# Transposing the convolved tiles of a state-space layer on VectorE and through memory instead of on TensorE

## The chip, the core and the metric

The kernel runs on one core of a Trainium2 chip. A core has TensorE (matrix products, with a queue for loading weights, PEld), VectorE (DVE), ScalarE (ACT), GpSimd (POOL) and SyncE (SP), which here issues nearly all DMA transfers from one queue; transfers are moved by 16 DMA engines. Matrix products are accumulated in PSUM, which has eight banks of 128 x 512 floats; everything else lies in SBUF. Each engine works through its own list of instructions in order, and waits at an instruction until what it needs is there. The metric is the time of one execution on the device in microseconds; lower is better. The text gives the median of several executions.

## What is computed

Two layers on `x` of shape (2, 512, 512): each adds `s * silu(f)` to `x`, where `s` is an attention-like part and `f` a feed-forward part. The change lies in the attention-like part of the second layer, a Mamba-2 block with 128 heads of 64 channels in 8 groups, state size 128 and chunks of 128 time steps:

```python
hBC = silu(causal_conv(hBC, conv_w, conv_b))         # 4 taps along time
hid, B, C = split(hBC)                               # hid: 128 heads x 64
hid_dt = hid * dt[..., None]
A_cs = cumsum(A * dt)                                # within a chunk
L = exp(segsum(A * dt))
M = einsum('cihn,cjhn->cijh', C, B) * L
Y_diag = einsum('cijh,cjhp->cihp', M, hid_dt)
states = einsum('clhn,hcl,clhp->chpn', B, exp(A_cs[-1] - A_cs), hid_dt)
prev_states = ...                                    # states carried from chunk to chunk
Y_off = einsum('clhn,chpn,hcl->clhp', C, prev_states, exp(A_cs))
y = (Y_diag + Y_off + Dp * hid) * silu(gate)
y = y * rsqrt(mean over the group of y*y + eps) * gnorm_w
out = x + y @ out_proj.T
```

The projections and the convolution are made with channels on the partitions and time along the row, since the taps run along time. The products with `M` and the sums for the states run over time, so they want `hid * dt` with time on the partitions. Between the two each 128 x 512 tile must be transposed, in four blocks of 128 x 128. That transpose is what is changed.

## The kernel before

The first 530 us make the first layer, the feed-forward parts, and the tables that the block needs. The rest (L1048 to L1985) is one loop over 64 steps, written out by hand in order: the program is recorded in the order of the Python calls, so the place of a call fixes the place of its instructions in each engine's list.

The work is cut into 16 units (group g, batch b; `u = 2g + b`) of 8 tiles each; a tile is 128 channels (two heads) by 512 time steps. A step handles two tiles, so a unit has four steps, called t = 0, 2, 4, 6 by the first tile's place in its unit. In step d four pairs of tiles are at work:

- `a` (tiles 2d, 2d+1): `products` (L1171), the two big sums with `M` and with the states; then `finish_y` (L1199) on VectorE (L1205, L1206).
- `n` (tiles 2d+2, 2d+3): the transposes on TensorE (`transposed`, L1226), the scaling by dt and by the decay (`values`, L1233: `hc` for the products, `hcd` for the states), the exponentials (`clamp` and `decays`, L1249 to L1269), the moments with B (`begun`, L1271, tile `pn`), the states of the four chunks (`states`, L1281: one copy on ScalarE, then four small VectorE instructions), and C times the decay on GpSimd (`starts`, L1299, tile `eb`).
- `h` (tiles 2d+4, 2d+5): projected on TensorE by a seven-product scheme (class `Values`), convolved on ScalarE and VectorE (`first_tap`, `taps`), then a silu on ScalarE (`silu`, L1589) at the end of the step, because silus and exponentials need a table load on ScalarE between them.
- `p` (tiles 2d-2, 2d-1): multiplied by the gate's silu on GpSimd (L1688) and squared (`square`, L1210: ScalarE squares, GpSimd adds).

At t = 0 the next unit's B and C are projected and convolved (`inner`); at t = 4 B is transposed on TensorE and multiplied with C (`inner_products`). In a unit's steps t = 2, 4, 6 the output product of the unit before is made on TensorE (class `Output`; VectorE adds each piece to `acc`, L1553, and the next piece goes into the same bank). For it GpSimd makes four sums of y (L1498) at t = 2 ahead of `starts`, and four at t = 4 behind them. The weights of the output are loaded once in a group (`load_out`, 2 MB, at t = 0 of a b = 1 unit), and four long sums of them are made on GpSimd (`sum_out`, L1093 to L1098): two at t = 0 and two at t = 2 of the b = 1 unit. At the end of a step GpSimd makes eight sums of the weights of the next step's projections (L581).

Loads for a step are issued on SP at its start, in this order: `load_sums` for two tiles (`cs`, which waits until the products have released a buffer), `load_starts` (`eb`), `load_gate` (`wg`), `load_hid` (`wh`), then `load_rest` (`el`).

The eight PSUM banks are: `pj` three (projections and gates), `tr` one (transposes, moments, B's transposes), `de` one (the exponentials), `of` one and `yy` two (output, products and others). The transposed tile is read by `values` right out of PSUM; the scale factors lie in SBUF.

## Time and profile before

Three runs took 2213.21, 2215.6 and 2215.95 us; the median is 2215.6 us. The profiled execution has a span of 2213.2 us, and its time is the same to the digit given, 2213.2. The granted TensorE clock is 1.000 throughout.

| engine | busy us | share of the span | instructions |
|---|---|---|---|
| TensorE | 2191.3 | 99% | 12460 |
| VectorE | 1513.8 | 68% | 2985 |
| ScalarE | 1299.4 | 59% | 2864 |
| GpSimd | 1321.7 | 60% | 1234 |

From 530 us on, in the loop, TensorE is busy 1675.2 of 1683 us, VectorE 1229.6, ScalarE 1151.2, GpSimd 1132.3, and the DMA engines 49%.

How to read it: in a line of a timeline stand the start in us, the time in us, the engine, the source line, the operation, the tile written and the tiles read, the shape, and how many instructions are merged; in square brackets the idle time before it and who ended it. Names are without their buffer numbers: `px` is a transposed tile in PSUM, `pjh` a projection of a tile, `gt` and `gty` of a gate, `of` and `ofy` an output product, `py` the products, `cs` the sums that become exponentials, `de` their bank, `s` and `wt` the sums for the output. A recorded time includes the end of the pipeline, so that the next instruction of an engine can start a little before the one ahead ends; start to start is what an instruction holds its engine.

### The profile page before, as it was taken

The numbers are of one execution on the slowest core, as the hardware profiler recorded it, in microseconds if no ns is written. First come the engines' busy times: TensorE is split into PE (matmuls) and PEld (weight loads), VectorE is DVE, ScalarE is ACT, GpSimd is POOL, SyncE is SP. The second block draws the span as 40 slices with busy tenths as digits, with TensorE's granted clock in tenths as the row PEclk, the third lists the DMA queues.
The fourth block names the chain that finished last, engine by engine and source line by source line (L and its number), as shares of the span: only waits on it lengthen the run. The fifth ranks groups of instructions, "written<-read, shape, count | busy, mean of one in ns | idle before, by whom it ended". The sixth has DMA issues, their size and how long they took to land.

```text
span 2213.2 us, 35453 instructions
## 1 busy us (share of the span) xinstructions
PE 2191.3 (99%) x12460; PEld 1712.6 (77%) x12460; DVE 1513.8 (68%) x2985; ACT 1299.4 (59%) x2864; POOL 1321.7 (60%) x1234
## 2 busy tenths in 40 slices
PE   8999999999999999999999999999999999999999
PEld 4545567765568888888888888888888888888877
DVE  5263577545777777777777677777777677777763
ACT  4131323214777667676767676767767676767671
POOL 4151523323457567776766686759576866766577
PEclk9999999999999999999999999999999999999999
DMA  4012266755544446444545454454446444544452
GB/s 174 1 58 75 80 226 221 255 195 195 176 143 129 148 140 190 133 135 124 167 133 148 152 175 128 134 162 129 134 141 187 138 145 124 167 124 133 141 187 97
DMA packets 195953, 323.51 MB, mean 146 GB/s; under 512 B 17728, under 2 KB 129984, under 8 KB 193344
## 3 DMA queue, kind: packets, MB, share of 16 engines
q1 hardware_dynamic: 189376, 300.28, 44.5%
q0 software_dynamic: 6400, 20.98, 2.5%
q8 instruction: 99, 1.62, 0.3%
q14 instruction: 78, 0.64, 0.1%
HBM read 294.45 MB, written 26.74 MB: 145 GB/s over the span
## 4 chain that ended last, share of the span: by engine, by line
PE 95%; DVE 2%; ACT 1%; DMA 1%; POOL 0%; issue 0%; SPq 0%; ACTq 0%; DVEq 0%
PE pjh L607 15%; PE of L1530 15%; PE gt L607 13%; PE py L1177 5%; PE pjbc L1139 5%; PE pf L1018 4%; PE pn L1276 4%; PE py L1186 4%; PE px L1230 3%; PE ofy L1530 2%; PE hu L361 2%; PE sh L522 2%; PE pg L607 2%; PE pu L607 2%; PE gty L607 2%; PE gt L1139 2%
## 5 line engine op out<-in xcount | busy, mean ns | idle before, releaser
L1301 POOL TENSOR_TENSOR eb<-CT,eb 128x768 f32<-128x768 f32 x128 | 230.0, 1818 | 342.9 <-DMA eb<-ea_d 287.1
L1254 ACT ACTIVATE cs<-cs,sl 128x128 f32<-128x128 f32 x1024 | 325.0, 390 | 0.6 <-DMA cs<-cs_d 0.6
L1158 DVE SCALAR_TENSOR_TENSOR hid<-pjh,cw,hid 128x511 f32<-128x511 f32 (+2 forms) x384 | 286.5, 746 | 43.1 <-ACT hid L1149 35.6
L1269 DVE TENSOR_TENSOR cs<-de,CB 128x512 f32<-128x512 f32 x256 | 175.4, 685 | 80.0 <-ACT de L1268 79.0
L1688 POOL TENSOR_TENSOR y<-y,sgt 128x512 f32<-128x512 f32 x124 | 176.1, 1440 | 11.6 <-ACT sgt L1410 9.7
L1177 PE MATMUL py<-cs,hc 128*64 128x128 f32 x2048 | 180.3, 276 | 0.0
L1222 POOL TENSOR_TENSOR sums<-sums,sq 128x512 f32<-128x512 f32 x110 | 140.1, 1273 | 61.3 <-ACT sq L1218 57.6
L1268 ACT ACTIVATE de<-cs 128x512 f32<-128x512 f32 x256 | 154.0, 602 | 28.9 <-DVE cs L1269 22.6
L1186 PE MATMUL py<-eb,st 128*64 128x128 f32 x1536 | 149.1, 273 | 0.0
L1289 DVE SCALAR_TENSOR_TENSOR st<-st,sl,pn 128x64 f32<-128x64 f32 x512 | 108.4, 275 | 59.4 <-ACT st L1285 59.4
L1553 DVE SCALAR_TENSOR_TENSOR acc<-of,rg,acc 128x256 f32<-128x256 f32 x188 | 90.2, 480 | 74.7 <-PE of L1530 74.4
L1354 ACT COPY hid<-pjh 128x256 f32<-128x256 f32 x171 | 63.6, 372 | 129.5 <-PE pjh L607 127.7
L1206 DVE SCALAR_TENSOR_TENSOR y<-hid,Dcol,y 128x512 f32<-128x512 f32 x128 | 133.8, 1045 | 4.5
L1177 PEld LDWEIGHTS py<-cs,hc 128*64 128x64 f32 x2048 | 121.5, 137 | 19.9 <-issue 18.1
L1205 DVE TENSOR_TENSOR y<-py,el 128x512 f32<-128x512 f32 x128 | 87.7, 685 | 57.1 <-PE py L1186 56.3
L1285 ACT COPY st<-pn 128x128 f32<-128x128 f32 x128 | 33.1, 264 | 153.3 <-PE pn L1276 153.3
L1530 PE MATMUL of<-wt,y 128*128 128x256 f32 x512 | 121.8, 381 | 0.0
L1139 PE MATMUL pjbc<-hT,wbc 128*128 128x512 f32 x256 | 117.4, 593 | 2.1 <-DVE BT L1158 1.3
L1530 PE MATMUL of<-wo,s 128*128 128x256 f32 x496 | 118.8, 382 | 0.0
L1276 PEld LDWEIGHTS pn<-hcd,Bs 128*128 128x128 f32 x768 | 104.7, 191 | 16.5 <-issue 11.3
L607 PE MATMUL pjh<-th,sh 128*128 128x256 f32 x456 | 117.3, 380 | 0.2 <-POOL sh L581 0.2
L607 PE MATMUL pjh<-hT,wh 128*128 128x256 f32 x456 | 117.2, 379 | 0.0
(356 smaller groups left out, 5518.7 us busy)
## 6 DMA issues: line engine op xcount, KB each, us to landing
cs<-cs_d SPq DMA_DIRECT2D x128, 512.0 KB, 4.3
eb<-ea_d SPq DMA_DIRECT2D x256, 192.0 KB, 6.0
wh<-in_in_wT SPq DMA_DIRECT2D x64, 512.0 KB, 9.2
wg<-in_in_wT SPq DMA_DIRECT2D x64, 512.0 KB, 7.4
el<-ea_d SPq DMA_DIRECT2D x256, 128.0 KB, 7.5
wo<-wo_d SPq DMA_DIRECT2D x16, 1024.0 KB, 8.4
wop<-in_out_wT SPq DMA_DIRECT2D x39, 256.0 KB, 2.8
wo_d<-wop POOLq DMA_DIRECT2D x39, 256.0 KB, 2.8
```

The costliest lines, as they stand in the source:

```text
L607: nc.tensor.matmul(ps, x[:, k, :], y[:, k, :], start=(first and k == 0), stop=(k == 1), skip_group_check=True,)
L1139: nc.tensor.matmul(ps, w_of(k), hT[:, k, bass.ts(b, S)], start=(k == 0), stop=(k == KD - 1))
L1158: nc.vector.scalar_tensor_tensor(dst[:, j:], ps[:, : S - j], cw[:, ct, KCONV - 1 - j : KCONV - j], dst[:, j:], ALU.mult, ALU.add,)
L1177: nc.tensor.matmul(py[bass.ts(hh, HP), bass.ts(c, P)], hc[:, c, bass.ts(hh, HP)], M[:, hh, bass.ts(c, P)], start=True, stop=(c == 0),)
L1186: nc.tensor.matmul(py[bass.ts(hh, HP), bass.ts(c, P)], st[:, c - 1, bass.ts(hh, HP)], cte[:, hh, bass.ts(c - 1, P)], start=False, stop=True,)
L1254: nc.scalar.activation(m[:, bass.ts(c, P)], m[:, bass.ts(c, P)], AF.Relu, bias=sls[g][:, 3, b * NCH + c, h0 + hh : h0 + hh + 1], scale=-1.0,)
L1268: nc.scalar.activation(pe, m, AF.Exp, scale=-1.0)
L1269: nc.vector.tensor_tensor(m, pe, CBs[s // GT].rearrange("p c i -> p (c i)"), ALU.mult)
L1276: nc.tensor.matmul(pn[:, c, :], Bss[s // GT][:, c, :], hcd[:, c, :], start=True, stop=True)
L1301: nc.gpsimd.tensor_tensor(eb_t[s], CTs[s // GT][:, P:].unsqueeze(1).to_broadcast([P, 2, S - P]), eb_t[s], ALU.mult,)
L1530: nc.tensor.matmul(ps, x[:, k, :], y[:, k, :], start=(first and k == 0), stop=(k == 3), skip_group_check=True,)
L1688: nc.gpsimd.tensor_tensor(y_of(s), y_of(s), sgs.pop(s), ALU.mult)
```

## The change

For all tiles but the first two, the transposes on TensorE are taken away. `turn` stands in their place, behind the silus of the step before: VectorE transposes the tile in blocks of 32 x 32 (one instruction for a tile of 128 x 512), which leaves each block in its band of 32 partitions; four DMA stores per pair, one for each band, write the blocks to their places in a scratch tensor in memory (pieces of 512 bytes), and in the next step `fetch` loads the pair back (pieces of 2 KB) into the tile it came from. The pair shares one SBUF tile with the squares (`sq`), which were two tiles before. `values` reads the tile from SBUF now, and because of the layout it takes four instructions instead of two. It stands later in VectorE's list, behind two exponentials' multiplies. The four VectorE instructions of the second tile's states move behind the transposes. B's transposes stay on TensorE. The bank `tr` is gone and `de` has two banks, which the exponentials, the moments, B's transposes and the mean of squares take in turn; two exponentials of a tile are issued one after the other on ScalarE, and their multiplies apart from them. On SP, `fetch` stands behind the `cs` loads, and `load_starts` and `load_out` move behind `fetch`, `load_gate` and `load_hid`.

```diff
+        def two_tiles(name):
+            return wk.tile([P, 2, S], F32, tag="sq", name=name, bufs=1)
+
+        def turn(ss, between=None):
+            if ss:
+                to = two_tiles(f"tn{ss[0]}")
+                for j, s in enumerate(ss):
+                    nc.vector.transpose(
+                        to[:, j, :].rearrange("p (q c e) -> p q c e", q=4, c=NCH),
+                        hid[s].rearrange("p (c q e) -> p q c e", c=NCH, q=4),
+                    )
+                    raw[s] = to[:, j, :]
+                    if between and j == 0:
+                        between()
+                dst = dram.tile([2, P, 4, P], F32, tag="tn_d", name=f"tn_d{ss[0]}", bufs=3)
+                for a in range(4):
+                    nc.sync.dma_start(
+                        dst[:, :, a, :].rearrange("j (q r) e -> r j q e", q=4),
+                        to[32 * a : 32 * a + 32].rearrange("r j (q e) -> r j q e", q=4),
+                    )
+                sent[ss[0]] = to, dst
+
+        def fetch(ss):
+            if ss:
+                to, src = sent.pop(ss[0])
+                nc.sync.dma_start(to, src.rearrange("j p a e -> p j (a e)"))
...
-                q = wk.tile([P, S], F32, tag="sq", name=f"sq{s}", bufs=2)
+                q = pairs[0][:, t % 2, :]
...
-            for dst, j, n in ((hc, 0, NCH), (hcd, 1, NCH - 1)):
-                nc.vector.tensor_tensor(
-                    dst.rearrange("p c (h d) -> p c h d", h=2),
-                    pxh[:, 0:n],
-                    pair(sls[g][:, j, b * NCH : b * NCH + n, h0 : h0 + 2]),
-                    ALU.mult,
-                )
+            for dst, j, n in (
+                (hc.rearrange("p c (a e) -> p a c e", a=4), 0, NCH),
+                (hcd.rearrange("p c (a e) -> p a c e", a=4), 1, NCH - 1),
+            ):
+                for h in range(2):
+                    two = slice(2 * h, 2 * h + 2)
+                    f = sls[g][:, j, b * NCH : b * NCH + n, h0 + h]
+                    f = f.unsqueeze(1).unsqueeze(3).to_broadcast([P, 2, n, 32])
+                    nc.vector.tensor_tensor(dst[:, two], src[:, two, 0:n], f, ALU.mult)
...
-            pe = psum.tile([P, S], F32, tag="de", name=f"de{s}_{hh}", bufs=1)
+            pe = psum.tile([P, S], F32, tag="de", name=f"de{s}_{hh}", bufs=2)
             nc.scalar.activation(pe, m, AF.Exp, scale=-1.0)
-            nc.vector.tensor_tensor(m, pe, CBs[s // GT].rearrange("p c i -> p (c i)"), ALU.mult)
+
+            def multiplied():
+                CB = CBs[s // GT].rearrange("p c i -> p (c i)")
+                nc.vector.tensor_tensor(m, pe, CB, ALU.mult)
+
+            return multiplied
...
-            tag, bufs = ("pj", 3) if spare else ("tr", 1)
+            tag, bufs = ("pj", 3) if spare else ("de", 2)
             pn = psum.tile([P, NCH - 1, P], F32, tag=tag, name=f"pn{s}", bufs=bufs)
...
             for s in n[1:]:
                 load_sums(s)
-            if b == 1 and t == 0 and 0 < g < NG:
-                load_out(g)
             for s in h[:1]:
                 load_sums(s)
-            for s in n:
-                load_starts(s)
+            fetch(n)
             if n:
                 load_gate(n[0] // 2)
             if h and h[0] // 2 < tiles // 2 - 1:
                 whs[h[0] // 2 + 1] = load_hid(h[0] // 2 + 1)
+            for s in n:
+                load_starts(s)
+            if b == 1 and t == 0 and 0 < g < NG:
+                load_out(g)
...
-                px = transposed(n[0])
                 hids.multiply(1, 5)
-                hcd = [values(n[0], px)]
-                decays(n[0], 0)
+                made_first = [exponentials(n[0], hh) for hh in range(2)]
+                made_first[0]()
                 hids.copy(0, 0)
+                made_second = exponentials(n[1], 0)
                 hids.multiply(2, 3)
                 hids.add(0, 0)
-                decays(n[0], 1)
+                made_first[1]()
+                hcd = [values(n[0])]
+                made_second()
+                hcd.append(values(n[1]))
                 starts(n[0])
                 output()
                 if projected is not None:
                     b_of = inner(projected, 0)
-                px = transposed(n[1])
                 hids.multiply(6)
                 if not late:
                     added()
-                hcd.append(values(n[1], px))
-                decays(n[1], 0)
...
-                states(n[1], pn)
+                first_state(n[1], pn)
                 if projected is not None:
                     first_tap(*c_of)
                 pss = squares()
                 gates.multiply(3)
                 silu()
-                gates.add(0, 1)
+                turn(h, lambda: gates.add(0, 1))
+                rest_of_states(n[1], pn)
                 output(int(t < 6))
```

`first_state` is the ScalarE copy of `states`, and `rest_of_states` its four VectorE instructions. The few steps that are written in another order (t = 2, 4, 6 of the first unit, t = 0, 4 of the last, and the head before the loop) are changed alike: `turn` behind `silu`, `values` from the fetched tile. In the tail, the last two squares take the tag `hc`.

## The prediction

> **What bounds the kernel now.** Read first the page's busy shares and its chain of work that ended last:
>
> ```profile
> PE 2191.3 (99%) x12460; PEld 1712.6 (77%) x12460; DVE 1513.8 (68%) x2985; ACT 1299.4 (59%) x2864; POOL 1321.7 (60%) x1234
> ...
> PE 95%; DVE 2%; ACT 1%; DMA 1%; POOL 0%; issue 0%; SPq 0%; ACTq 0%; DVEq 0%
> ```
>
> TensorE is never idle and is the path. Second, the busy times of four consecutive steps, from one start of the products to the next (t=4 and 6 of a unit, then 0 and 2 of the next, a b=1 unit):
>
> ```profile
> core 0: us, PE busy (x) PEld busy (x) DVE busy (x) ACT busy (x) POOL busy (x), PEclk, DMA share, GB/s
> 1209.85:1237.48 27.63, 27.63 (x186) 24.68 (x185) 19.80 (x39) 18.23 (x43) 20.38 (x21) 1.00 0.42 125
> 1237.48:1262.05 24.57, 24.57 (x166) 21.72 (x165) 17.77 (x35) 15.74 (x36) 11.41 (x11) 1.00 0.48 140
> 1262.05:1287.47 25.42, 25.42 (x157) 19.65 (x156) 19.32 (x39) 17.67 (x40) 16.38 (x12) 1.00 0.67 218
> 1287.47:1313.99 26.52, 26.52 (x173) 23.15 (x173) 21.18 (x43) 21.22 (x48) 26.20 (x24) 1.00 0.49 140
> ```
>
> An average would hide the last line: at t=2 GpSimd is busy 26.20 of 26.52 us and VectorE 21.18. Third, the timelines of TensorE, VectorE and GpSimd there:
>
> ```profile
> 1306.10 1.89 PE L1530 MATMUL of<-wt,s 128*128 128x256 f32 x8
> ...
> 1308.86 0.47 DVE L1553 SCALAR_TENSOR_TENSOR acc<-of,rg,acc 128x256 f32<-128x256 f32 x1
> ...
> 1309.39 1.99 PE L1530 MATMUL of<-wo,s 128*128 128x256 f32 x8
> ...
> 1294.56 2.50 POOL L1688 TENSOR_TENSOR y<-y,sgt 128x512 f32<-128x512 f32 x2
> 1297.01 2.37 POOL L1096 TENSOR_TENSOR wt<-wo 128x1024 f32<-128x1024 f32 x1
> 1299.33 1.27 POOL L1498 TENSOR_TENSOR s<-y,y 128x512 f32<-128x512 f32 x1
> ...
> 1304.37 2.35 POOL L1098 TENSOR_TENSOR wt<-wo,wt 128x1024 f32<-128x1024 f32 x1
> 1306.68 3.59 POOL L1301 TENSOR_TENSOR eb<-CT,eb 128x768 f32<-128x768 f32 x2
> ```
>
> The product at 1309.39 writes the bank that VectorE's sum read until 1309.33: TensorE leaves VectorE no slack there, so VectorE's lateness in the second half of t=2 is TensorE's. GpSimd works without a gap. Fourth, what VectorE pays beside GpSimd when both its inputs lie in SBUF:
>
> ```profile
> 508.97 0.42 DVE L891 TENSOR_TENSOR it<-it,pu 128x256 f32<-128x256 f32 x1
> 509.31 1.52 DVE L891 TENSOR_TENSOR it<-it,uq 128x256 f32<-128x256 f32 x1
> ...
> 509.28 1.26 POOL L570 TENSOR_TENSOR th<-hT,th 128x512 f32<-128x512 f32 x1
> ```
>
> One multiply, one size: 0.42 us with an input in PSUM, 1.52 us with both in SBUF. It sat out GpSimd's 1.26 us instruction.
>
> **The change, part by part.** S is a step's start (first product on TensorE); for t=2 it is 1287.47 in the trace. Both "before" and sum are of the profiled execution: its span and its time are 2213.2 us, 2.4 us under the median 2215.6.
>
> *TensorE, removed.* The two groups of four transposes hold the stream this long:
>
> ```profile
> 1240.69 0.66 PE L1230 MATMUL px<-ident,hid 128*128 128x128 f32 x4
> 1241.18 1.03 PE L607 MATMUL pjh<-hT,wh 128*128 128x256 f32 x4
> ...
> 1246.36 0.60 PE L1230 MATMUL px<-ident,hid 128*128 128x128 f32 x4
> 1246.80 1.03 PE L607 MATMUL pjh<-th,sh 128*128 128x256 f32 x4
> ```
>
> 0.49 + 0.44 = 0.93 us to the next group. The first pair of tiles keeps them, 63 pairs lose them: −58.6 us if nothing else moves.
>
> *Banks.* The freed bank becomes a second one for exponentials. ScalarE waited 22.6 us in all for that bank, off the path: 0. The moments (pn) and B's transposes share these two; each bank's reader is over a half step earlier: 0.
>
> *VectorE, added.* Per tile two multiplies from PSUM (recorded 0.68 and 0.55 us, 0.60 and 0.46 start to start) become four from SBUF, two of 256 columns (0.42, start to start 0.33) and two of 192 (between the 0.275 of 64 columns and 0.42; I take 0.27): +0.14 per tile, uncontended. The block transpose of 128x512 is in no row. Below it lies the scaling of 128x512 from one SBUF source, 0.51 us (L838); above it two passes of a 128x512 multiply, 1.37. I take one such pass, 0.685 recorded and 0.60 to the next start, the nearest kind. Per step +0.28 + 1.20 = 1.5 us on 17.8 to 21.2.
>
> [...]
>
> *The trip through memory.* Let T be the end of the second transpose. Four stores issue at 0.34 to 0.4 us each; stores of 128 KB land in 1.7 (output), of 256 KB in 2.0 to 3.1. So memory is written at T+4. The load back stands behind both cs loads, whose second goes out at S+3.1 because it waits for the products, so it issues at the later of S+3.6 and T+4. Its 512 KB land like cs (4.3) to wg (7.4); I take 5, near cs, since only cs is ahead. For t=4, 6, 0 T is between S−0.5 and S+0.4 (VectorE's last sums now end about there), so the tile is back at S+8.6 to 9.5, its eight multiplies done by S+12.7, n0's by S+11. TensorE's moments need n0's at S+12.7 (1223.49−1209.85−0.93): covered, by 1 to 1.7 us. GpSimd meanwhile waits for eb (5.71 us of such waiting in the first step above), and eb now comes later still, behind the load back, wg and wh: at about S+13.5, not S+9.4. That costs only at t=4, where its queue (starts, four sums, squares) ends at S+25.3 and the transposes, which reuse the squares' tile, wait 2.4 us for it; T is then S+0.2 of the next step, as used. load_out behind eb: 2 MB wanted at S+18.7, landed at about S+18: 0. SP waits for T with the next cs loads queued behind; before, they waited until S+1.6 for TensorE: 0 except at t=2.
>
> *t=0 into t=2.* At t=0 ScalarE ends with C's first tap, a table load and B's silu, so the tile's silus end at S'+0.9 and S'+1.4 (S' the next start; 1288.35 and 1288.9 against 1287.47). VectorE now stands there waiting for them, and behind the transposes are queued the states of n1, which ended 0.5 us before S': now S'+3.4. TensorE reads the last at S'+2.9 (1290.36): 0.5 us, 15 times: +8. C's taps (2.2 us) come after, so the y's begin at S'+5.6 instead of 2.7, T is S'+2.5, memory written S'+6.5, tile back S'+11.6. Then 1.2 + 0.6 + 1.2 + 0.6 us of multiplies: the states begin at S'+15.3. Before, it was 15.3 with 0.93 us of transposes ahead. So VectorE is 0.9 to 1.1 late where there is no slack: +8 over eight b=0 units.
>
> *t=2 of the b=1 units (7 of them).* By my count GpSimd's row there starts 2 us earlier (eb is no longer behind wo): y's from S+5, wt to S+10, the four sums to S+15, wt, then eb's. The eight multiplies arrive at S+11.6 in the midst of it, each with both inputs in SBUF. They alternate with GpSimd's instructions, waiting about 0.6, 1.1, 1.1, 2.2, then 1.2, 1.7, 1.1, 0.6 = 9.6 us. With what the b=0 units lose that is over 10 us a step, straight onto TensorE: I take 10, +70. Bounds: 0 if GpSimd is not there then; 14 if the y's wait as well.
>
> Sum: −58.6 + 8 + 8 + 70 = +27; 2213.2 + 27 = 2240, and with 2.4 to the median 2243.
>
> [...]
>
> **The rivals.**
> *Faster.* The multiplies don't meet GpSimd at t=2: the tile is back before the sums begin, or they win the shared access at once. Then 2215.6 − 58.6 + 16 = 2173. For it: in three steps of four GpSimd is idle at that time. Against it: 26.20 busy of 26.52, and the 1.52 us row. The point is 42/7 = 6 us of waiting in each of the seven steps: under that the change wins.
> *Memory too late everywhere.* If the load back takes wh's 9.2 instead of 5, tiles come at S+13 in all steps, and 47 more steps lose 1 to 2.7 us: 2243 + 47 to 127 = 2290 to 2370. Against: wh and wg are 1 KB pieces at the queue's end, this is 2 KB near its front.
> *A wash.* Six of ten microseconds of those waits: within 0.2% of 2215.6, about what a measurement can tell from no change.
> *Transposes at the upper bound (1.37)*: +0.7 each, on the path at t=2 alone, 16 x 1.4 = 22: 2265, inside the likeliest's range.
>
> **How the numbers follow.** GpSimd against the multiplies: 0.47, alone 2218 to 2285. Faster: 0.33. Too late everywhere: 0.15. A wash: 0.05. The prediction is 2243. The range 2160 to 2310 leaves out about a tenth on either side: the faster case where the two small losses at t=2 and t=0 vanish too (2157), and the later half of the third. Faster 0.34, same 0.05, slower 0.61.
>
> **What would show it.** TensorE's transposes gone and 0.93 us a step with them; 126 block transposes near 0.69; the load back landing 8.6 to 9.5 us after S, 11.6 at t=2; multiplies at 0.42 in most steps and 1 to 2.5 in t=2 of b=1 units, with TensorE waiting there by some 10 us and nowhere else by over 1. It is wrong if those seven steps keep their length, or if the waits stand at the load back in every step.

## The result

The changed kernel takes 2324.97 us (median of four executions, 2318.68 to 2332.32), the kernel before 2215.37 us: a ratio of 1.0493, 95% interval 1.0469 to 1.0518. Slower was the likelier side of the forecast, but the time lies above the range of 2160 to 2310. The profiled execution took 2328.39 us, with a span of 2326.7 and a mean granted TensorE clock of 0.990 (1.000 before).

The page of the changed kernel, the busy times and the chain that ended last:

```profile
PE 2189.5 (94%) x11956; PEld 1673.2 (72%) x11956; DVE 1667.5 (72%) x3367; ACT 1307.0 (56%) x2864; POOL 1335.5 (57%) x1234
...
PE 40%; DMA 19%; DVE 18%; POOL 11%; ACT 5%; issue 4%; SPq 2%; DVEq 0%; POOLq 0%; ACTq 0%
```

TensorE has 504 instructions less (126 tiles of four) and is hardly less busy in sum: behind waits its products are drawn out (the moments in a timeline below take 1.65 us instead of 0.83). The chain, 95% TensorE before, now runs through DMA, VectorE and GpSimd for about half of the span.

The same four steps in a row as in the prediction (t=4, 6, then 0 and 2 of a b=1 unit):

```profile
core 0: us, PE busy (x) PEld busy (x) DVE busy (x) ACT busy (x) POOL busy (x), PEclk, DMA share, GB/s
...
1258.09:1285.50 27.41, 27.06 (x177) 23.89 (x177) 19.62 (x42) 16.56 (x38) 16.03 (x14) 1.00 0.56 164
1285.50:1310.34 24.84, 24.23 (x158) 20.91 (x157) 19.21 (x44) 17.57 (x40) 16.65 (x17) 1.00 0.65 180
1310.34:1336.51 26.17, 25.12 (x149) 18.86 (x148) 19.67 (x43) 18.50 (x42) 14.80 (x12) 1.00 0.78 251
1336.51:1373.83 37.32, 28.27 (x166) 23.35 (x165) 34.22 (x55) 20.64 (x46) 30.75 (x27) 0.95 0.41 120
```

The last step is 10.8 us longer than before, and VectorE is busy 34.22 us in it instead of 21.18. The other three should be 0.93 us shorter; they are 0.2 us shorter to 0.75 us longer. The sums over all 63 steps (from the first product of a step to that of the next) show the same two things and a third:

| steps | before, us | after, us | forecast difference | measured |
|---|---|---|---|---|
| t=2 of b=1 units, from the second group on (7) | 187.0 | 255.0 | +67 | +68.0 |
| the other t=2 steps behind the first unit (8) | 212.2 | 215.0 | +4 | +2.8 |
| t=0, 4, 6 behind the first unit (44) | 1135.7 | 1158.5 | -41 | +22.8 |
| the first unit (4) | 82.0 | 100.7 | -3 | +18.7 |
| ahead of and behind the steps | 596.3 | 597.5 | 0 | +1.2 |
| sum (the spans) | 2213.2 | 2326.7 | +27 | +113.5 |

The forecast column sorts the terms of the prediction by the place where they fall. So the seven steps came as forecast. Of the 86 us that are missing 64 lie in the 44 steps that were thought to be covered, and 22 in the first unit.

The timelines of VectorE, GpSimd and TensorE in the last of the four steps:

```profile
1348.51 3.23 DVE L1281 TENSOR_TENSOR hc<-tn,sl 128x256 f32<-128x256 f32 x2 [2.30 <-DMA tn<-tn_d]
1351.66 2.74 DVE L1281 TENSOR_TENSOR hcd<-tn,sl 128x192 f32<-128x192 f32 x2
1354.33 0.68 DVE L1311 TENSOR_TENSOR cs<-de,CB 128x512 f32<-128x512 f32 x1
1354.93 3.38 DVE L1281 TENSOR_TENSOR hc<-tn,sl 128x256 f32<-128x256 f32 x2
1358.23 3.84 DVE L1281 TENSOR_TENSOR hcd<-tn,sl 128x192 f32<-128x192 f32 x2
...
1350.02 1.44 POOL L1548 TENSOR_TENSOR s<-y,y 128x512 f32<-128x512 f32 x1
1351.54 1.32 POOL L1548 TENSOR_TENSOR s<-s,y 128x512 f32<-128x512 f32 x1
...
1355.50 2.53 POOL L1098 TENSOR_TENSOR wt<-wo,wt 128x1024 f32<-128x1024 f32 x1
1357.98 3.87 POOL L1351 TENSOR_TENSOR eb<-CT,eb 128x768 f32<-128x768 f32 x2
...
1355.07 1.65 PE L1320 MATMUL pn<-hcd,Bs 128*128 128x128 f32 x6 [4.92 <-DVE cs L1311]
```

The eight multiplies take 13.2 us here and 2.75 us in a quiet step: they go in turn with GpSimd's instructions. TensorE's moments wait 4.92 us: for the first four of them, until 1354.40, and 0.6 us more for the exponential's multiply (`cs`) that stands behind these and frees the bank. In the same step of the kernel before, with the tile read from PSUM, VectorE's four multiplies were not drawn out, though GpSimd worked without a gap there too:

```profile
1293.93 0.68 DVE L1240 TENSOR_TENSOR hc<-px,sl 128x512 f32<-128x512 f32 x1
1294.54 0.54 DVE L1240 TENSOR_TENSOR hcd<-px,sl 128x384 f32<-128x384 f32 x1
...
1297.01 0.68 DVE L1240 TENSOR_TENSOR hc<-px,sl 128x512 f32<-128x512 f32 x1
1297.61 0.55 DVE L1240 TENSOR_TENSOR hcd<-px,sl 128x384 f32<-128x384 f32 x1
```

And the step behind it (t=4, S = 1373.83), where GpSimd is not in the way: SP's queue, VectorE and TensorE.

```profile
1373.36 1.85 SPq L1228 DMA_DIRECT2D tn_d<-tn  x4
...
1375.88 1.54 SPq L1114 DMA_DIRECT2D cs<-cs_d  x2
1378.65 0.37 SPq L1237 DMA_DIRECT2D tn<-tn_d  x1
...
1384.71 0.76 DVE L1281 TENSOR_TENSOR hc<-tn,sl 128x256 f32<-128x256 f32 x2 [2.82 <-DMA tn<-tn_d]
...
1391.88 0.47 DVE L1603 SCALAR_TENSOR_TENSOR acc<-of,rg,acc 128x256 f32<-128x256 f32 x1
...
1392.41 1.99 PE L1580 MATMUL of<-wo,y 128*128 128x256 f32 x8 [0.50 <-DVE acc L1603]
```

The second block transpose ends at 1373.33 (T). The load back is issued 5.3 us later (4.4 us in the median of the units 1 to 14), and the tile is there 6 us after that, at S+10.9; VectorE stands 2.82 us. TensorE feels it 7 us further on: the output's sum comes late, and the bank with it. Over the whole run VectorE stands 153.6 us at the load back (56 times).

### The profile page after: what moved, and what is told of

Its sections match the earlier page's. It is cut to its first block, busy times and chain, and to the rows that moved or that the text cites. A ratio compares the mean times of both kernels' runs of the same rounds, so it can differ in the third digit from the quotient of the medians.

```text
span 2326.7 us, 35554 instructions
## 1 busy us (share of the span) xinstructions
PE 2189.5 (94%) x11956; PEld 1673.2 (72%) x11956; DVE 1667.5 (72%) x3367; ACT 1307.0 (56%) x2864; POOL 1335.5 (57%) x1234
## 4 chain that ended last, share of the span: by engine, by line
PE 40%; DMA 19%; DVE 18%; POOL 11%; ACT 5%; issue 4%; SPq 2%; DVEq 0%; POOLq 0%; ACTq 0%
DMA tn<-tn_d 9%; PE of L1580 5%; PE pf L1018 4%; DMA eb<-ea_d 4%; DVE hcd L1281 4%; DVE hc L1281 3%; PE pjh L607 3%; DMA tn_d<-tn 3%; PE gt L607 3%; DVE hid L1158 2%; PE pjbc L1139 2%; PE sh L522 2%; PE hu L361 2%; POOL s L1548 2%; PE pg L607 2%
## 5 line engine op out<-in xcount | busy, mean ns | idle before, releaser
L1351 POOL TENSOR_TENSOR eb<-CT,eb 128x768 f32<-128x768 f32 x128 | 232.9, 1836 | 553.0 <-DMA eb<-ea_d 432.7
L1281 DVE TENSOR_TENSOR hc<-tn,sl 128x256 f32<-128x256 f32 x252 | 129.8, 556 | 153.6 <-DMA tn<-tn_d 153.6
L1177 PE MATMUL py<-cs,hc 128*64 128x128 f32 x2048 | 181.5, 276 | 11.9 <-DVE CB L1503 11.9
L1320 PE MATMUL pn<-hcd,Bs 128*128 128x128 f32 x768 | 115.0, 289 | 56.9 <-DVE cs L1311 37.2
L607 PE MATMUL gt<-th,wg 128*128 128x256 f32 x456 | 119.8, 385 | 27.1 <-ACT sgt L1449 13.5
L607 PE MATMUL pjh<-th,wh 128*128 128x256 f32 x456 | 123.5, 395 | 3.8 <-ACT hid L1404 3.6
L1149 ACT ACTIVATE hid<-pjh,cb,cw 128x512 f32<-128x512 f32 x128 | 93.3, 773 | 59.6 <-DVE pjh L1409 52.3
L1281 DVE TENSOR_TENSOR hcd<-tn,sl 128x192 f32<-128x192 f32 x252 | 125.2, 537 | 0.0
L607 PE MATMUL pjh<-hT,wh 128*128 128x256 f32 x456 | 123.0, 392 | 0.0
L1219 DVE STREAM_TRANSPOSE tn<-hid 128x512 f32<-128x512 f32 x126 | 88.1, 701 | 48.4 <-POOL sums L1253 35.1
```

Of the source, the lines that this page charges most:

```text
L607: nc.tensor.matmul(ps, x[:, k, :], y[:, k, :], start=(first and k == 0), stop=(k == 1), skip_group_check=True,)
L1177: nc.tensor.matmul(py[bass.ts(hh, HP), bass.ts(c, P)], hc[:, c, bass.ts(hh, HP)], M[:, hh, bass.ts(c, P)], start=True, stop=(c == 0),)
L1281: nc.vector.tensor_tensor(dst[:, two], src[:, two, 0:n], f, ALU.mult)
L1320: nc.tensor.matmul(pn[:, c, :], Bss[s // GT][:, c, :], hcd[:, c, :], start=True, stop=True)
L1351: nc.gpsimd.tensor_tensor(eb_t[s], CTs[s // GT][:, P:].unsqueeze(1).to_broadcast([P, 2, S - P]), eb_t[s], ALU.mult,)
```

## The experiments

The mean lengths of steps in the twelve middle units, in us, are read from each kernel's trace in the same way (first product to first product); "first" is the sum of the first unit's four steps. Six of the seven t=2 steps of b=1 units lie in the twelve; the seventh is in the last unit.

| kernel | t=0 | t=2, b=0 | t=2, b=1 | t=4, b=0 | t=4, b=1 | t=6, b=0 | t=6, b=1 | first | time, us |
|---|---|---|---|---|---|---|---|---|---|
| before | 25.42 | 26.52 | 26.52 | 27.63 | 27.63 | 24.57 | 24.57 | 82.0 | 2215.4 |
| after | 25.74 | 26.94 | 36.90 | 27.43 | 28.22 | 25.34 | 25.41 | 100.7 | 2325.0 |
| one operand | 24.75 | 27.57 | 35.53 | 26.79 | 27.42 | 25.06 | 25.91 | 93.6 | 2290.3 |
| no trip | 24.59 | 29.09 | 35.40 | 26.79 | 26.80 | 24.11 | 23.85 | 102.9 | 2279.9 |
| neither | 24.59 | 26.34 | 33.20 | 26.79 | 26.79 | 23.94 | 23.74 | 96.8 | 2241.3 |
| transposes back | 25.42 | 27.25 | 26.73 | 27.63 | 27.63 | 24.57 | 24.57 | 82.0 | 2225.5 |
| hybrid | 25.70 | 26.73 | 26.74 | 27.00 | 28.99 | 24.72 | 25.46 | 82.0 | 2237.5 |
| quiet GpSimd | 25.46 | 27.16 | 26.97 | 27.02 | 28.43 | 25.36 | 25.48 | 89.8 | 2255.1 |
| one store, four loads | 26.61 | 27.14 | 37.15 | 27.59 | 28.99 | 25.84 | 25.47 | 88.1 | 2352.4 |
| that, hybrid, later | 25.97 | 28.16 | 27.85 | 28.31 | 28.83 | 25.66 | 26.96 | 82.2 | 2284.5 |
| load back first | 25.35 | 26.97 | 27.62 | 26.80 | 27.54 | 24.94 | 27.64 | 82.0 | 2245.2 |
| that, later | 26.28 | 27.64 | 27.15 | 27.81 | 28.57 | 25.74 | 26.09 | 82.2 | 2270.0 |
| eb early | 26.86 | 29.48 | 27.16 | 29.70 | 30.72 | 24.86 | 24.82 | 83.3 | 2298.4 |
| eb and weights early | 26.96 | 29.09 | 27.44 | 29.94 | 30.06 | 24.70 | 24.94 | 83.2 | 2293.6 |

The theory after the result: two losses, GpSimd beside the multiplies in the seven steps, and the late tile everywhere else. The rivals: the late tile makes both, or VectorE's longer list is the bound.

### One operand from SBUF

```diff
-                    nc.vector.tensor_tensor(dst[:, two], src[:, two, 0:n], f, ALU.mult)
+                    nc.vector.tensor_scalar(dst[:, two], src[:, two, 0:n], 1.0, None, ALU.mult)
```

> The changed kernel, but the eight multiplies of a step read one operand from SBUF instead of two: they multiply by the constant 1, so the scale factors are left out of the computation. Same number of instructions and elements, same trip through memory.
> Theory (two separate losses: the multiplies stand still beside GpSimd's instructions in the seven t=2 steps of b=1 units, which last 36.9 us in the profile against 26.5 before; and the load back comes 2 to 2.5 us later than forecast in every step): only the first loss goes. The seven steps fall to 27 to 28.5 us, 60 to 70 us in all; the first unit's last multiply (2.5 us beside GpSimd's) gives 5 to 10 more; 2245 to 2262 us.
> Rival (the late tile alone makes both, the stretched multiplies are only seen because TensorE stands still anyway): under 15 us change, 2310 or more.
> Rival (VectorE's longer list): 2300 or more, since the multiplies get shorter by less than 0.1 us each outside the seven steps.

2290.3 us, a ratio of 1.0331 [1.0305, 1.0356]. None of the three had it. The seven steps get only 1.4 us shorter: the multiply by a constant, with its single SBUF operand, is held up by GpSimd as well (0.286 us in the median, 2.36 us at most; rows of a like version below), so the experiment did not take the meeting away. But the multiplies alone are shorter, 0.286 and 0.253 us instead of 0.419 and 0.351, together 0.92 us a step, and t=0 falls by 0.99 us, t=4 by 0.6 to 0.8. At these two places VectorE's time behind the late tile goes into the step almost one to one; at t=6 (25.06 and 25.91 us, from 25.34 and 25.41) it does not.

### No trip through memory

```diff
-                for a in range(4):
-                    nc.sync.dma_start(
-                        dst[:, :, a, :].rearrange("j (q r) e -> r j q e", q=4),
-                        to[32 * a : 32 * a + 32].rearrange("r j (q e) -> r j q e", q=4),
-                    )
...
-                nc.sync.dma_start(to, src.rearrange("j p a e -> p j (a e)"))
```

> The changed kernel without the four stores and the load back: the multiplies read the tile right behind the block transposes, so its blocks are not in their places (the placing is left out of the computation). VectorE's instructions are the same.
> Theory (two separate losses): the waits at the load back (153.6 us of VectorE in the profile) go, and with them about 1.3 us in each of some 50 steps and 15 to 20 us in the first unit; the seven t=2 steps of b=1 units keep most of their excess, because GpSimd works there without a gap wherever the multiplies fall: 32 to 35 us each. 2215 to 2245 us.
> Rival (the late tile alone): the seven steps lose their excess too, 2150 to 2175.
> Rival (VectorE's longer list, 2 us more in each step, is what TensorE waits for): 2290 or more.

2279.9 us, 1.0277 [1.0248, 1.0306]. In t=0, 4 and 6 the theory's loss is gone: 24.59, 26.80 and about 24.0 us, 0.5 to 0.84 less than before, with the same list on VectorE, whose length alone is therefore not what TensorE waited for. The seven steps stay at 35.4, just above the theory's 32 to 35. The total is 35 us above the theory's range, because the multiplies, now ready earlier, meet GpSimd in steps where the trip had kept them apart: t=2 of the b=0 units, where they now take 3 us more than when GpSimd is idle, goes up from 26.9 to 29.1, the first unit to 102.9.

### Neither

Both edits together.

> Both of the last two: multiplies with one operand from SBUF (factors left out) and no trip through memory (placing left out). What is left of the change is TensorE without its transposes, the block transposes on VectorE, the banks and the order.
> Theory (the two losses are all): TensorE is the bound again, 63 x 0.93 us below before, and at most 10 us above that: 2155 to 2170 us, the granted clock 1.000.
> Rival (VectorE's longer list): 2190 or more, with TensorE waiting for VectorE in most steps.

2241.3 us, 1.0107 [1.0092, 1.0122], 70 us above the theory's upper end, so "the two losses are all" was tested badly: one of them was still there. VectorE and GpSimd in a t=2 step of a b=1 unit:

```profile
891.86 2.21 DVE L1273 TENSOR_SCALAR hc<-tn 128x256 f32<-128x256 f32 x2
893.99 1.49 DVE L1273 TENSOR_SCALAR hcd<-tn 128x192 f32<-128x192 f32 x2
...
896.01 2.04 DVE L1273 TENSOR_SCALAR hc<-tn 128x256 f32<-128x256 f32 x2
897.97 4.18 DVE L1273 TENSOR_SCALAR hcd<-tn 128x192 f32<-128x192 f32 x2
...
892.60 1.32 POOL L1540 TENSOR_TENSOR s<-y,y 128x512 f32<-128x512 f32 x1
894.00 1.37 POOL L1540 TENSOR_TENSOR s<-s,y 128x512 f32<-128x512 f32 x1
```

Four pairs that take 0.4 to 0.5 us alone take 9.9 us in all. The excess left over before sits where GpSimd meets the multiplies: 6.7 us in each of the seven steps and 15 us in the first unit. In the other steps the time is 0.2 us (t=2) to 0.84 us below before: this is the gain that the change has when nothing waits.

### TensorE's transposes put back

The transposes and the two multiplies from PSUM stand where they stood before; the rest of the change stays (TensorE's branch):

```diff
+                if by_tensor(d):
+                    px = transposed(n[0], False, "de")
+                    hids.multiply(1, 5)
+                    hcd = [values(n[0], px)]
+                    decays(n[0], 0)
...
-                turn(h, lambda: gates.add(0, 1))
+                if by_tensor(d + 1):
+                    gates.add(0, 1)
+                else:
+                    turn(h, lambda: gates.add(0, 1))
```

> The changed kernel with the 126 tiles transposed on TensorE again and multiplied right out of PSUM, at the places of before and with the two multiplies of before; the transposes take one of the two exponential banks in turn. The other edits stay: the two banks, B's transposes and moments in them, the squares' tile, the order of the loads, the states of the second tile at the step's end.
> Theory (those edits cost nothing): within 5 us of before, 2211 to 2221 us.
> Rival (the order of the loads or the banks take part of the loss): 2225 or more, with TensorE waiting for exponentials or for eb.

2225.5 us, 1.0034 [1.0021, 1.0048], at the border between the two: 7 us above before, nearly all at t=2 of the b=0 units (27.25 against 26.52), where the second tile's transposes wait 0.53 us for an exponential in the shared banks. In every other kind of step the length is that of before to 0.21 us. The other edits are not where 110 us went.

### Hybrid: TensorE where the meeting is

```diff
+        def by_tensor(d):
+            u, t = divmod(2 * d, GT)
+            return (u % 2 == 1 and t == 2) or u == 0 or plain(d)
```

> The changed kernel, but with TensorE's transposes and multiplies from PSUM, at the places of before, in the steps where the profile shows VectorE's multiplies beside a busy GpSimd or TensorE with nothing else to do: t=2 of the b=1 units, the first unit, t=0 and 4 of the last. The trip through memory stays in the other 51 steps. Nothing is left out.
> Theory (GpSimd meets the multiplies when they read SBUF alone, and not when they read PSUM, as L1240 did beside the same row of GpSimd before; the rest is the late tile): the seven steps fall from 36.9 to about 26.7 us, 70 us in all, the first unit by 19, the last unit's two by 6: 2222 to 2240 us.
> Rival (the seven steps are long because the trip's traffic or the new order delays them, not the multiplies' reads): 2260 or more.

2237.5 us, 1.0088 [1.0073, 1.0103], as the theory had it: the seven steps at 26.74, the first unit at 82.0. Read from PSUM the multiplies take 0.68 and 0.55 us there, the length of before.

### GpSimd kept quiet

```diff
+            if g > 0 and part > 0:
+                return
...
+                if self.g > 0 and self.b == 0 and p == 0:
+                    self.s[p] = a11, a12, a22
+                    return
```

> The changed kernel with GpSimd kept quiet in the seven t=2 steps of b=1 units: the first four sums of y there and the last two sums of the output's weights are not made, and the output products read unsummed quarters in their place (that part of the computation is left out). VectorE's multiplies, their operands, the trip and TensorE's instructions stay.
> Theory (meeting GpSimd is the seven steps' loss): the multiplies there take 0.35 to 0.45 us each instead of 1.4 to 1.9, the steps 27 to 28.5 us instead of 36.9, all other steps as they were: 2250 to 2265 us.
> Rival (the late tile): the steps keep at least 33 us, 2300 or more.

2255.1 us, 1.0163 [1.0147, 1.0179], inside the theory's range. VectorE in one of the seven steps:

```profile
1105.78 0.76 DVE L1283 TENSOR_TENSOR hc<-tn,sl 128x256 f32<-128x256 f32 x2 [2.54 <-DMA tn<-tn_d]
1106.45 0.62 DVE L1283 TENSOR_TENSOR hcd<-tn,sl 128x192 f32<-128x192 f32 x2
...
1107.59 0.75 DVE L1283 TENSOR_TENSOR hc<-tn,sl 128x256 f32<-128x256 f32 x2
1108.26 0.62 DVE L1283 TENSOR_TENSOR hcd<-tn,sl 128x192 f32<-128x192 f32 x2
```

The same instructions with the same operands and the same late tile, and without GpSimd's row: 2.75 us instead of 13.2, the step 26.97 us instead of 36.90. This settles the seven steps. The first unit, which the edit doesn't touch, was 89.8 us here and 100.7 in the profile of the changed kernel: its loss differs between these two runs.

### One store, four loads

```diff
-                for a in range(4):
-                    nc.sync.dma_start(
-                        dst[:, :, a, :].rearrange("j (q r) e -> r j q e", q=4),
-                        to[32 * a : 32 * a + 32].rearrange("r j (q e) -> r j q e", q=4),
-                    )
+                nc.sync.dma_start(dst, to.rearrange("p j (q e) -> p j q e", q=4))
...
-                nc.sync.dma_start(to, src.rearrange("j p a e -> p j (a e)"))
+                for q in range(4):
+                    nc.sync.dma_start(
+                        to[32 * q : 32 * q + 32].rearrange("r j (a e) -> r j a e", a=4),
+                        src[:, :, q, :].rearrange("(a r) j e -> r j a e", a=4),
+                    )
```

> The changed kernel with the trip cut differently: one store of the whole pair as it lies (pieces of 4 KB), and four loads, one for each band of 32 partitions, that put the blocks in their places (pieces of 512 bytes). The cs loads go out while the store lands. Nothing else changes, nothing is left out.
> Estimate from the trace: store issued and landed T+3.2 instead of T+5.3, four loads issued by T+5, back 3 to 4 us later at T+8.5 instead of T+11 (T: end of the second block transpose).
> Theory (the late tile costs some 1.3 us in each of about 50 steps): VectorE's wait at the load back falls from about 3 us to about 1 us, those steps by 0.6 to 1 us: 2275 to 2297 us.
> Rival (the tile's time is covered and the steps' excess comes from VectorE's longer list): 2315 or more.
> The loads of 512-byte pieces may land later than I take them; then the tile is no earlier, and so is the time.

2352.4 us, 1.0615 [1.0593, 1.0637]: later, not earlier. Its DMA list:

```profile
tn_d<-tn SPq DMA_DIRECT2D x63, 512.0 KB, 2.9
tn<-tn_d SPq DMA_DIRECT2D x252, 128.0 KB, 5.4
```

The store lands in 2.9 us, as taken, but each load of 128 KB in pieces of 512 bytes takes 5.4 us, against 6.0 us for one of 512 KB in pieces of 2 KB, and the four are issued 0.65 to 0.8 us apart. In one t=4 step the tile is back at S+12.6, and VectorE's wait there is 4.55 us; in all it is 188.3 us. The time moves with the tile's lateness, in the direction that the theory asks for.

Combined with the hybrid, and with the multiplies moved behind the second tile's exponentials:

```diff
-                    hcd = [values(n[0])]
...
-                    hcd.append(values(n[1]))
...
                 decays(n[1], 1)
+                hcd = hcd or [values(s) for s in n]
```

> The first and third of these together (TensorE's transposes in the steps named, one store and four loads in the others), and in the others the eight multiplies stand later in VectorE's list, behind the second tile's exponentials, the output's sum and B's taps, so that VectorE works while the tile comes. Nothing is left out.
> Theory: of the 51 steps that still go through memory most gain the 0.83 us that they gained without the trip: 2215 - 42 + up to 20 for t=2 of the b=0 units and what lateness is left: 2172 to 2195 us, faster than before by 1 to 2 per cent.
> Rival (the trip can't be covered within a step): 2210 or more.

It took 2284.5 us, 1.0314 [1.0265, 1.0362]. The rival had it: the moments on TensorE now wait for the multiplies, 49 times and 51.9 us in all.

### The load back ahead of the second cs load

On top of the hybrid:

```diff
             for s in n[1:]:
                 load_sums(s)
+            if not by_tensor(d):
+                fetch(n)
             for s in h[:1]:
                 load_sums(s)
-            if not by_tensor(d):
-                fetch(n)
```

> The version with TensorE's transposes in the seven steps, the first unit and t=0 and 4 of the last (2237 us), with one edit more: on SP the load back stands ahead of the second cs load, which is for the next step, instead of behind it. Nothing is left out.
> Theory (the late tile is what the other steps lose): the load back then has 512 KB less ahead of it in the queue and comes back 1 to 2 us earlier, at S+9 to S+10 instead of S+11; VectorE's wait there falls from 137 us to 60 to 90, and the steps gain 0.3 to 0.8 us each: 2200 to 2225 us.
> Rival (bandwidth is shared by whatever is under way, and the order on the queue changes nothing): 2232 to 2242.
> Rival (the cs load that is now later makes ScalarE's clamps late): over 2245.

2245.2 us, 1.0128 [1.0111, 1.0145]. The first half of the theory held: the load back takes 4.5 us instead of 6.0, VectorE's wait falls from 137.1 to 64.0 us, t=4 of the b=0 units is at 26.80 in every unit, the length that it has without the trip, and t=0 falls from 25.70 to 25.35. But t=6 of the b=1 units goes up from 25.46 to 27.64, and the sum is 8 us worse. VectorE and TensorE at the start of such a step (S = 1140.62):

```profile
1141.37 0.71 DVE L1219 STREAM_TRANSPOSE tn<-hid 128x512 f32<-128x512 f32 x1 [4.07 <-POOL sums L1253]
...
1144.06 0.68 DVE L1516 TENSOR_TENSOR CB<-pc,upper 128x512 f32<-128x512 f32 x1
...
1144.79 1.12 PE L1177 MATMUL py<-cs,hc 128*64 128x128 f32 x8 [2.42 <-DVE CB L1516]
1145.69 0.64 PE L1186 MATMUL py<-eb,st 128*64 128x128 f32 x4
```

A third loss, which the prediction had half: the block transposes share the squares' tile, so they wait for GpSimd's sums of squares at t=4; those stand behind eb, whose loads the change puts at the end of SP's queue. Behind the transposes VectorE has the mask of the next unit's B and C, and the products of t=6 need that. The changed kernel shows it too, smaller: 35.1 us of transposes waiting for those sums, and 15.3 us of products' weight loads waiting for the mask. The second rival's number, over 2245, is met at its edge, but not its reason: ScalarE's waits for cs fall from 76.2 us in the hybrid to 42.4.

With the multiplies later in VectorE's list as well (the second diff of the section before):

> The same, and in the steps that go through memory the eight multiplies stand behind the second tile's exponentials, the output's sum and B's taps in VectorE's list, so that VectorE has work while the tile comes. Nothing is left out.
> Theory: VectorE's wait for the tile nearly gone (under 30 us); at t=0 and t=4 less time lost than in the version without the move, 2190 to 2215 us.
> Rival (the moments on TensorE wait for the multiplies instead, at S+12.7): no gain over the version without the move, or a loss of up to 20 us.

2270.0 us, 1.0242 [1.0227, 1.0257]. Here the rival came out, with a loss of 25 us where it said up to 20: VectorE waits for ScalarE's exponentials instead of the tile (135.5 us), and the moments on TensorE wait for the multiplies (65.2 us of their weight loads).

### eb back in its place

```diff
             if not by_tensor(d):
                 fetch(n)
+            for s in n:
+                load_starts(s)
             for s in h[:1]:
                 load_sums(s)
...
-            for s in n:
-                load_starts(s)
```

> The version with the load back ahead of the second cs load (2245 us), with the eb loads again ahead of the second cs load, wg and wh, right behind the load back, instead of behind them all. Nothing is left out.
> Theory (in that version the eb loads, which the change puts at the queue's end, hold GpSimd up until its sums of squares at t=4 are late; the block transposes, which use the squares' tile, wait 4.07 us for them, VectorE's mask of the next unit's C and B stands behind them, and the products of t=6 wait 2.42 us for it): eb lands 3 to 4 us earlier, those waits go, t=6 of the b=1 units falls from 27.5 to 24.5 us or less, and with t=0 and t=4 already at the length that they have without the trip the time is 2185 to 2205 us, faster than before.
> Rival (eb ahead of wg and wh makes the weights' sums on GpSimd and the projections late instead): 2225 or more.

2298.4 us, 1.0373 [1.0344, 1.0401], far above the theory. The rival's number holds, but not its reason: TensorE's products wait 4.7 us in all for the weights' sums, and 5.6 us without this edit. The chain through the squares is gone as forecast: t=6 of the b=1 units falls from 27.64 to 24.82. But t=2 of the b=0 units and t=4 grow by 2.5 to 3.2 us each, and t=0 by 1.5. VectorE, GpSimd and TensorE at t=4:

```profile
1144.57 3.39 DVE L1294 TENSOR_TENSOR hc<-tn,sl 128x256 f32<-128x256 f32 x2
1147.89 2.75 DVE L1294 TENSOR_TENSOR hcd<-tn,sl 128x192 f32<-128x192 f32 x2
...
1143.91 3.77 POOL L1364 TENSOR_TENSOR eb<-CT,eb 128x768 f32<-128x768 f32 x2 [2.81 <-DMA eb<-ea_d]
1147.64 1.44 POOL L1561 TENSOR_TENSOR s<-y,y 128x512 f32<-128x512 f32 x1
...
1151.09 3.44 PE L1593 MATMUL of<-wt,y 128*128 128x256 f32 x8 [3.04 <-DVE acc L1616]
```

An eb that lands early wakes GpSimd just when the multiplies run: over the 49 steps they take 287 us, and 141 us without this edit. The late eb of the changed kernel, which looks like a cost (432.7 us of GpSimd's waiting), is what keeps the two engines apart in most steps.

The output's weights earlier too:

```diff
             for s in n:
                 load_starts(s)
+            if b == 1 and t == 0 and 0 < g < NG:
+                load_out(g)
```

> The same, and the 2 MB of the output's weights again ahead of the second cs load, wg and wh (seven times, at t=0 of b=1 units), behind eb. Nothing is left out.
> Theory: GpSimd's two long sums at the end of those steps no longer wait for the weights (0.9 to 1.8 us), the eight sums behind them and the next step's start come earlier: 3 to 10 us less than without this edit.
> Rival (2 MB ahead of the second cs load, wg and wh make these late): 5 to 30 us more.

2293.6 us, 1.0347 [1.0332, 1.0363], 5 us less, inside the theory's range, with intervals that overlap; it doesn't change the picture.

No version that was run beats the kernel before. The nearest are the one with the transposes back on TensorE (+0.34%) and the hybrid (+0.88%).

## Why the prediction was wrong, step by step

*TensorE's 0.93 us.* Right but for its size. Where nothing waits a step is 0.83 or 0.84 us shorter. The rest is at the first product group behind `products`: it now holds the stream 0.96 us (1377.04 to 1378.00), and 0.87 us before, when it stood behind the transposes. 63 steps make -53, not -58.6.

*VectorE's prices.* Right. The block transpose takes 0.70 us (0.685 was taken, 0.62 start to start against 0.60), the multiplies 0.419 and 0.351 us. The row of the nearest kind was a good guide.

*The trip: "covered, by 1 to 1.7 us".* This is the step that failed. The leg to memory was nearly right: the stores issue 0.46 us apart (0.34 to 0.4 taken) and land in 2.5 us in the median (2.0 to 4.4), and in the units 1 to 14 memory is written at T+4.3 in the median (4.0 to 5.6), where T+4 was taken. The leg back was not: the load takes 6.0 us (4.4 to 8.2), not 5, with two cs loads still under way ahead of it, as the run with one of them behind it shows (4.5 us). And T itself is later than taken for two of the tiles, at S+0.7 for those of t=6 (S+0.2 taken) and at S+1.3 for those of t=0 (at most S+0.4). So the tile is back at S+11.1 at t=4 and S+11.5 at t=6 and 0 (medians), 2 to 2.5 us later than the text had it, and at S+12.0 at t=2, 0.4 us later. The 5 us came from the lower half of rows from 4.3 to 7.4, and the lateness is more than the whole slack of 1 to 1.7 us.

*What the lateness costs.* The prediction looked at the moments (due at S+12.7), and in the t=4 step shown they are late by only 0.1 us. The cost comes behind them, since VectorE takes its list in order. In the units 1 to 14 TensorE's products wait at t=0 8.6 us for the gates' sums, and at t=4 5.2 us for the output's sums, which free their bank, and 2.9 us for the moments; at t=6 they wait 3.7 us for the output's sums and 11.9 us for the mask, of which the next paragraph tells. The rival "memory too late everywhere" had the late tile right, though not its cause (9.2 us for the load back), and its 1 to 2.7 us a step hold the 1.45 us that the 44 steps lost on the forecast ((22.8 + 41) / 44); it had 0.15 of the chance. That its time of 2290 to 2370 holds the measured one is in part luck: 22 us of the excess lie in the first unit, for which it had no term, and some of the rest is the mask's.

*The squares' tile.* The wait of the block transposes at t=4 was forecast as 2.4 us and is 2.04 and 2.20 us in two such steps. What was not followed is the instruction queued behind them, the mask, and the products of t=6 that need it: this is a second step that failed, with the 11.9 us above. "T is then S+0.2, as used" went on to the trip and forgot the rest of VectorE's list.

*t=0 into t=2.* +4 forecast, +2.8 measured, in eight steps. That the number is near is luck: the block transposes end at S+1.6, not S+2.5, the list of TensorE's waits has none for the states (0.5 us each was taken), and the moments wait instead, 3.7 us in the seven b=0 steps.

*The seven steps.* Right in place, cause and size: 26.52 - 0.93 + 0.5 + 10 = 36.1 us forecast, 36.90 measured; 9.6 us of waiting in the multiplies forecast, 10.4 measured in the step shown. The quiet GpSimd shows the cause. Two things in the 36.90 had no place in that sum, so that it comes out this close is partly luck: VectorE's 2.30 us of waiting for the tile ahead of the multiplies, and the clock, as told below. The reason given ("both inputs in SBUF") is too narrow, as told below.

*The first unit.* It has no term in the prediction, only the 0.93 us a step and one t=2 loss. In its steps SP's first store stands ahead of cs loads and waits for the transposes (cs goes out at 564.4, 8 us into the first step), and its long last multiplies stand beside eb (2 of them 3.83 us). It cost 6 to 19 us in the runs where it kept the trip, but 21 and 15 us in the two without it, so the stores are not the whole of it. Its loss goes with the length of its multiplies: they take 11.0 us in the two runs that lost least (7.8 and 6.1 us), 20.6 in the changed kernel (18.7) and 25.5 in the one without the trip (20.9). What makes the 6 to 8 us of those two runs was not tested. "0 except at t=2" for what is queued behind the stores was read from the steady steps.

*Banks, load order.* With TensorE's transposes back they cost 7 us at most, in a place where the changed kernel has no transposes; taken as 0. "Each bank's reader is over a half step earlier" does not hold for the moments, though: their bank's reader is the `cs` multiply right behind the first four multiplies, and in the seven steps its 0.6 us end their wait.

## What to carry to other kernels

Before an operand moves from PSUM to SBUF, lay GpSimd's timeline beside the place where VectorE will read it: the same multiplies cost 2.75 or 13.2 us by that alone, and an engine kept idle by a late load can be what protects them (141 us for them with a late eb, 287 with an early one). Hold the slack of a trip through memory against the spread of the rows from which its legs are taken, here 1 to 1.7 us against rows from 4.3 to 7.4; and when it is less, follow everything queued behind the waiting instruction, not only its first reader. When two engines compete, moving a load earlier can cost more than the wait that it removes: here some 20 us were cut from one chain, and over 70 added where the two engines then met.

## What the runs showed of the hardware

Which VectorE instructions GpSimd holds up. The changed kernel's block transposes (shortest, median and longest of 126), and the multiplies of the version without the trip and with one operand ("neither"), tiles from SBUF and the first two tiles from PSUM:

```profile
L1219 DVE STREAM_TRANSPOSE tn<-hid x126: 670/700/715, 559.7 to 2252.2; 128x512 f32<-128x512 f32 x126
```

```profile
L1273 DVE TENSOR_SCALAR hc<-tn x252: 276/286/2142, 570.5 to 2181.0; 128x256 f32<-128x256 f32 x126
...
L1273 DVE TENSOR_SCALAR hc<-px x4: 415/415/415, 548.1 to 549.6; 128x256 f32<-128x256 f32 x4
```

A block transpose reads and writes SBUF and none of the 126 is drawn out, though 99 of them ran beside GpSimd's sums for 0.3 us or more. A multiply by a constant with one SBUF operand is: 2142 ns instead of 286. From PSUM it takes 415 ns, more than from SBUF.

The clock. In the version with the load back first, around the products that waited 2.42 us:

```profile
core 0: us, PE busy (x) PEld busy (x) DVE busy (x) ACT busy (x) POOL busy (x), PEclk, DMA share, GB/s
...
1141.00:1144.70 3.70, 1.37 (x26) 1.13 (x22) 3.33 (x10) 2.28 (x7) 3.62 (x6) 1.00 0.20 40
1144.70:1148.00 3.30, 3.21 (x29) 2.88 (x29) 1.50 (x3) 3.27 (x7) 3.22 (x5) 0.50 0.92 231
```

Behind the wait the granted clock is 0.50 for 3.3 us, and the products' groups start 0.43 us apart instead of 0.22. So the wait cost TensorE some 1.6 us on top of its 2.42 (an estimate: 3.3 us at 0.50). It lies in a stretch of 3.70 us with TensorE busy for 1.37.

The changed kernel pays the same behind the ten longest waits of its loop, 3.31 to 4.92 us: the mean granted clock is 0.50 to 0.77 over the 2.5 us behind each. Behind its waits from 0.86 to 2.32 us, and behind the 0.50 us in the t=4 step shown, it is 1.00, but for one of 1.91 us (until 2269.69), 0.9 us of work behind another of 1.35, with 0.50. In the step of the first timelines, behind the 4.92 us:

```profile
core 0: us, PE busy (x) PEld busy (x) DVE busy (x) ACT busy (x) POOL busy (x), PEclk, DMA share, GB/s
...
1354.00:1360.00 6.00, 4.93 (x19) 4.43 (x20) 6.00 (x5) 0.79 (x2) 6.00 (x5) 0.72 0.06 19
```

Its mean clock of 0.990 over 2326.7 us makes some 23 us (an estimate from these two numbers). They lie in six of the seven steps (0.95 in the one shown), in the first unit (0.82 in its first step) and in the last unit (0.93 from 2265 to 2290 us), and the prediction had no term for them. How much of them the time lost is not shown, since TensorE waits again behind them.
